# A graph layer on one core: a slot's rows and terms are made two and four chunks earlier, the list's words are packed in fewer VectorE instructions, and VectorE takes a share of the one-hots from the list's making on

## The chip, the cores and the metric

The kernel runs on one core of one Trainium2 chip. The core has five engines with a queue each: PE (TensorE, matmul), DVE (VectorE), ACT (ScalarE), POOL (GpSimd) and SP (SyncE, which only issues transfers). Each engine works off its own queue strictly in order, and an instruction whose input is not there holds up everything behind it in that queue. The metric is the device time of one execution in microseconds.

## The reference

```python
def _L0_gnn_ref(x, src, dst, theta_w, theta_b, phi_w, phi_b):   # x (6250, 256), 100000 edges sorted by dst
    x_src = x[src]
    x_dst = x[dst]
    theta_x = (x_dst - x_src) @ theta_w.T + theta_b
    phi_x = x_src @ phi_w.T + phi_b
    e = jax.nn.relu(theta_x + phi_x)
    out = jax.ops.segment_max(e, dst, num_segments=x.shape[0])
    return jnp.where(jnp.isfinite(out), out, 0.0)
x = _layernorm(x + _L0_gnn_ref(...), axis=-1)
```

The sum inside the relu splits into a term of the edge's target, and B[src] with B = x (phi - theta)^T. So the kernel makes the table B once (`b_rows` in DRAM), takes for every node the maximum of B over its incoming edges, and adds the rest at the end.

## The kernel before

The maxima are made in three ways, by three engines, at the same time.

*Part 1* (618 nodes, 81 steps): POOL gathers rows of B for 128 chunks of the sorted edges, and DVE runs a running maximum over them, one `scalar_tensor_tensor` of 128x256 a step (L696, helper `run_steps`). Results go to `maxima_1` (SP, L711).

*Slots* (the other 5632 nodes, 44 to a partition): the rows of B are cut into 17 slots of 383. In each slot every node may take one of its edges; `choice` (L1020 on, DVE, two slots a call) picks it for all nodes. The chosen row numbers are turned by PE (L1053), copied by ACT (L1055) and stored (SP, L1056, `chosen_rows`). Later PE fetches the chosen rows of a slot by matmul with one-hot matrices: `slot_halves(s, c)` does chunk c (1024 nodes, the sixth 512) of slot s. For a chunk, SP loads `want` (L1094); the one-hots `hot` are made block by block, three blocks, either by DVE in one comparison (L1100) or by ACT in an Abs for each block (L1102) and one Relu over all of ACT's blocks (L1105). `dve_hots[0]` says how many blocks DVE makes: 0 at first, 1 from late in the list's making on, 0 again near the end. PE then multiplies (L1113), 12 matmuls for each of two halves of 512-wide columns, from `terms`, which is the slot's rows `raw` (loaded by SP, L1078, one buffer) split into a rounded part (ACT, L1082) and its rest (DVE, L1083); `slot_terms` does this at the head of a slot's chunk 0. `terms` and `hot` have two buffers each, PSUM three. The result is copied to `acc` in slot 0 (ACT, L1122) and merged by maximum in the others (DVE, L1124). Chunks are dealt out in halves by `fetch_parts` and `fetch_half`.

*List* (part 2): edges that no slot took are packed into a list, 256 steps of 128 rows. `list_pieces` makes it on DVE: which table places are left over (L1213, L1215), a running count (L1216), sums over partitions by two PE matmuls (L1151, L1152), the words (node, row and distance to move in one integer, L1225 to L1237), eleven rounds of moves that close the gaps (L1244 to L1254), the store (L1263), and three gathers that fetch each partition its run (L519). After each `yield` of `list_pieces` the program emits a group of part 1 and a chunk, or a chunk alone; so the program order of that stage is: a piece of the list, eight steps of part 1, a chunk. Then POOL gathers the list's rows (L526 from `list_src`), each gather followed by a `pause` iota; DVE runs the list's steps two groups of eight behind, and `halves_until` spreads the remaining halves evenly over the list steps, so that 12 halves are left for the end (`SPREAD` 0.97: the last of the others is emitted at step 248 of 256). With `pinned` set, DVE's order of steps and of L1124 is the program's. The ends of part 1's chunks are merged by `tails_1` and `heads_1` (PE transposes L905 and L914, DVE L907 and L910, ACT L916).

At the end POOL gathers the nodes' maxima (44 gathers), PE makes the targets' term, and DVE and ACT do the layer norm.

The order on each engine is made when the program is built: a scheduler takes instructions by program order where they are ready by its reckoning, so an instruction can stand ahead of others that were written earlier. Where the code says `behind_in_order`, the order is forced.

## Time and profile before

| | us |
|---|---|
| three runs | 739.37, 734.26, 736.09 (median 736.09) |
| the profiled execution, its own time | 738.83 |
| its span, first to last instruction | 737.0 |
| busy in the span: PE, DVE, ACT, POOL | 661.5, 630.5, 532.7, 529.1 |
| mean granted TensorE clock | 0.955 of full speed |
| edge table and choice on DVE; PE makes B | 0 to 118 |
| the list's making on DVE, chunks on the side | 118 to 214 |
| the list is stored and its runs fetched | 214 to 228 |
| list gathers, list steps and 148 halves | 228 to 651 |
| the nodes' maxima, the end | 651 to 737 |

Times in the profile are us from the span's start, busy times are the length of an instruction from its start to its end; instructions of one engine are pipelined and overlap a little, so that the next starts before the one ahead has ended. A wait stands in square brackets behind the instruction, with what ended it. "PE x24" are matmuls: 24 make one full chunk, 12 a narrow one.

### The profile page before, as it was taken

The numbers are of one execution on the slowest core, as the hardware profiler recorded it, in microseconds if no ns is written. First come the engines' busy times: TensorE is split into PE (matmuls) and PEld (weight loads), VectorE is DVE, ScalarE is ACT, GpSimd is POOL, SyncE is SP. The second block draws the span as 40 slices with busy tenths as digits, with TensorE's granted clock in tenths as the row PEclk, the third lists the DMA queues.
The fourth block names the chain that finished last, engine by engine and source line by source line (L and its number), as shares of the span: only waits on it lengthen the run. The fifth ranks groups of instructions, "written<-read, shape, count | busy, mean of one in ns | idle before, by whom it ended". The sixth has DMA issues, their size and how long they took to land.

```text
span 737.0 us, 9895 instructions
## 1 busy us (share of the span) xinstructions
PE 661.5 (90%) x2908; PEld 536.1 (73%) x2908; DVE 630.5 (86%) x1193; ACT 532.7 (72%) x611; POOL 529.1 (72%) x730
## 2 busy tenths in 40 slices
PE   5989978679697999999999999999999988979990
PEld 3878756567475888888888888888888876758880
DVE  7999998999996678988989888888888984697885
ACT  1445788788697676967869687876877878852685
POOL 6810477888315848888888888888888888438880
PEclk9999998889798999999999999999999998989995
DMA  8997553737456547777787968786867675555874
GB/s 260 313 360 289 191 165 108 261 101 229 156 194 207 179 143 223 247 217 260 222 277 217 354 218 272 249 312 223 263 211 252 210 243 177 164 187 172 269 279 192
DMA packets 60879, 167.06 MB, mean 227 GB/s; under 512 B 11896, under 2 KB 21905, under 8 KB 54673
## 3 DMA queue, kind: packets, MB, share of 16 engines
q1 hardware_dynamic: 39717, 107.15, 41.6%
q0 software_dynamic: 18976, 52.35, 24.1%
q10 hardware_dynamic: 2124, 6.84, 2.5%
q8 instruction: 25, 0.41, 0.2%
q14 instruction: 37, 0.30, 0.1%
HBM read 102.94 MB, written 63.36 MB: 226 GB/s over the span
## 4 chain that ended last, share of the span: by engine, by line
PE 63%; DVE 11%; DMA 7%; ACT 7%; POOL 6%; issue 6%; SPq 0%; DVEq 0%; POOLq 0%; ACTq 0%
PE ps_f L1113 56%; PE ps_b L791 4%; POOL g L526 4%; DMA x_columns<-x_t 3%; DVE g L696 2%; ACT hot L1102 2%; ACT hot L1105 2%; DMA g<-maxima,place 2%; POOL pause L496 1%; DVE wide L1032 1%; DMA dst_w<-list_words,run_start 1%; DVE words L1244 1%; DVE acc L1124 1%; DMA w_in<-in_L_gnn_theta_w_dram 1%; ACT x_t L779 1%
## 5 line engine op out<-in xcount | busy, mean ns | idle before, releaser
L1113 PE MATMUL ps_f<-hot,terms 128*128 128x512 f32 x2156 | 519.9, 402 | 28.0 <-ACT hot L1105 22.0
L1113 PEld LDWEIGHTS ps_f<-hot,terms 128*128 128x128 f32 x2156 | 412.7, 194 | 128.8 <-ACT hot L1105 31.6
L526 POOL DMA_INDIRECT g<-b_rows,list_src x256 | 258.2, 1009 | 61.0 <-issue 37.3
L1102 ACT ACTIVATE hot<-want,minus_row 128x1024 fp32r<-128x1024 f16 (+1 forms) x224 | 229.0, 1071 | 97.7 <-PE ps_f L1113 97.7
L1124 DVE TENSOR_TENSOR acc<-acc,ps_f 128x1024 f32<-128x1024 f32 x192 | 215.8, 1129 | 69.4 <-PE ps_f L1113 68.6
L1105 ACT ACTIVATE hot<-hot 128x2048 fp32r<-128x2048 f32 (+2 forms) x102 | 196.4, 1925 | 2.5
L696 DVE SCALAR_TENSOR_TENSOR g<-g,caps 128x256 f32<-128x256 f32 x335 | 161.1, 481 | 2.1
L526 POOL DMA_INDIRECT g<-b_rows,src x65 | 89.4, 1376 | 62.8 <-DMA b_rows<-b_sb 43.0
L496 POOL IOTA pause<- 128x160 f32 x312 | 96.9, 311 | 2.3
L791 PE MATMUL ps_b<-weights,x_t 128*128 128x256 f32 x260 | 60.9, 388 | 2.8 <-ACT x_t L779 2.4
L526 POOL DMA_INDIRECT g<-maxima,place x44 | 42.7, 971 | 27.1 <-DMA maxima<-g 20.2
L791 PEld LDWEIGHTS ps_b<-weights,x_t 128*128 128x128 f32 x260 | 48.9, 194 | 11.3 <-ACT x_t L779 5.2
L1100 DVE TENSOR_SCALAR hot<-want,row_id 128x1024 fp32r<-128x1024 f16 (+1 forms) x70 | 52.1, 745 | 0.3 <-issue 0.3
L1363 PE MATMUL ps_e<-weights,kept 128*128 128x256 f32 x176 | 41.6, 379 | 0.0
L1393 ACT ACTIVATE squares<-x_f,r 128x256 bf16<-128x256 f32 x49 | 24.2, 494 | 20.6 <-DVE r L1390 20.6
L1363 PEld LDWEIGHTS ps_e<-weights,kept 128*128 128x128 f32 x176 | 33.4, 190 | 4.3
L794 ACT COPY b_sb<-ps_b 128x512 f32<-128x512 f32 (+1 forms) x25 | 14.4, 578 | 23.4 <-PE ps_b L791 16.8
L779 ACT COPY x_t<-ps_xt 128x512 f32<-128x512 f32 (+1 forms) x33 | 18.5, 588 | 13.1 <-PE ps_xt L776 7.8
L526 POOL DMA_INDIRECT g<-in_x_dram,src x16 | 23.1, 1444 | 5.4 <-issue 4.1
L1408 ACT ACTIVATE x_f<-x_f,r 128x256 f32<-128x256 f32 x41 | 21.4, 588 | 6.8 <-DVE r L1400 3.9
L1373 DVE TENSOR_TENSOR g<-g,ps_e 128x512 f32<-128x512 f32 x22 | 15.1, 686 | 8.7 <-DMA g<-maxima,place 3.5
L519 POOL DMA_INDIRECT dst_w<-list_words,run_start x3 | 3.1, 1048 | 25.8 <-DMA list_words<-work 25.5
(255 smaller groups left out, 429.6 us busy)
## 6 DMA issues: line engine op xcount, KB each, us to landing
maxima<-g SPq DMA_DIRECT2D x42, 1024.0 KB
want<-chosen_rows SPq DMA_DIRECT2D x85, 256.0 KB
x_q<-in_x_dram SPq DMA_DIRECT2D x12, 512.0 KB
b_rows<-b_sb ACTq DMA_DIRECT2D x12, 512.0 KB
x_columns<-x_t SPq DMA_DIRECT2D x22, 256.0 KB
kept<-x_columns SPq DMA_DIRECT2D x11, 512.0 KB
raw<-b_rows SPq DMA_DIRECT2D x16, 256.0 KB
g<-b_rows,list_src POOLq DMA_INDIRECT x256, 4.3
```

The source lines that it names most:

```text
L496: return nc.gpsimd.iota(t, pattern=[[step, t.shape[1]]], base=base, channel_multiplier=per_partition, allow_small_or_imprecise_dtypes=True,)
L526: one = nc.gpsimd.indirect_dma_start(out=to, out_offset=None, in_=table, in_offset=bass.IndirectOffsetOnAxis(ap=offsets, axis=0))
L696: one = nc.vector.scalar_tensor_tensor(g[:, k, :], last[part], caps[:, t : t + 1], g[:, k, :], op0=ALU.min, op1=ALU.max)
L779: nc.scalar.copy(x_t[:, :w], ps[:, :w])
L791: nc.tensor.matmul(ps[:, h, :], x_t[:, h, k, :], weights[:, k, 0, :], start=(k == 0), stop=(k == KC - 1))
L1100: nc.vector.tensor_scalar(hot[:, b, :], want, row_id[:, b : b + 1], None, op0=ALU.is_equal)
L1102: nc.scalar.activation(hot[:, b, :], want, AF.Abs, bias=minus_row[:, b : b + 1], scale=1.0)
L1105: nc.scalar.activation(apart, apart.bitcast(FP), AF.Relu, bias=1.0, scale=-1.0)
L1113: nc.tensor.matmul(ps[:, w : w + 512], terms[:, part, b, h * P : (h + 1) * P], hot[:, b, w : w + 512], start=(i == 0), stop=(i == n - 1),)
L1124: one = nc.vector.tensor_tensor(to, to, ps, op=ALU.max)
L1363: nc.tensor.matmul(a[:, i, :], x_t[:, 2 * i + c, :], weights[:, c, 1, :], start=False, stop=(i == w - 1 and c == KC - 1))
L1393: nc.scalar.activation(squares, x_f[:, k, :], AF.Square, bias=mean[:, k : k + 1], scale=1.0, accum_out=var[:, k : k + 1])
```

## The change

Seven edits, of which some lie far from each other in the program.

1. `slot_terms` becomes a generator in two steps. The loads of the next slot's `raw` are issued at chunk 2 of the slot before (`ROWS_AT`), and its two parts of `terms` are made at chunk 4 (`TERMS_AT`). Only slot 0 still does both at its chunk 0.
2. `dve_hots[0] = DVE_HOTS` is set ahead of the list's making instead of at its 14th piece: 13 chunks of the list's making and three behind it get one of their three blocks of one-hots from DVE.
3. The list: "empty" in one instruction instead of "left over" in two, the words in two instead of five, the owner in one instead of two. The addition of the node's number to the words (DVE, L1228) goes to POOL, as an addition and a cast, right behind the edge table.
4. `choice`: the first slot writes `unused` itself instead of multiplying it in. The memsets of `unused` (what is left of it) and of `words` go from DVE to POOL.
5. The sums' matmuls (L1151, L1152 before) are written one piece later, and are forced behind the latest chunk's last product.
6. The transposes of part 1's carries (L914 before) and their copy go from `tails_1` into `heads_1`, where they are forced behind the latest product as well.
7. In the last list groups `halves_until` is no longer called, and the last `fetch_parts` takes all that is left.

Its core, cut:

```diff
+ROWS_AT = 2
+TERMS_AT = 4
...
+    def heads_1(capped):
         carry = misc()
         for k in range(KC):
-            nc.tensor.transpose(carry[:, k * P : (k + 1) * P], capped[:, k, :], ident)
+            one = nc.tensor.transpose(carry[:, k * P : (k + 1) * P], capped[:, k, :], ident)
+            behind_in_order(one, latest_product[0], "slots ahead of the heads")
...
-    nc.vector.memset(unused, 1)
+    nc.gpsimd.memset(unused[:, CHOICE_R * TILES :], 1)
...
-        nc.vector.memset(words[:, : TR - W], EMPTY)
+        nc.gpsimd.memset(words[:, : TR - W], EMPTY)
...
+        by_nodes = words.rearrange(by_node, r=R)
+        nc.gpsimd.tensor_tensor(by_nodes, by_nodes, node_part.to_broadcast([P, TILES, R]), op=ALU.add)
+        nc.gpsimd.tensor_copy(word, words)
...
         terms = terms_of[s] = slots.tile([P, PARTS, KB, D], FR, name="terms")
...
-        if c == 0:
-            slot_terms(s)
+        if c == 0 and s == 0:
+            for _ in slot_terms(s):
+                pass
+        if c == ROWS_AT and s + 1 < NS:
+            terms_ahead[0] = slot_terms(s + 1)
+            next(terms_ahead[0])
+        if c == TERMS_AT and s + 1 < NS:
+            next(terms_ahead[0])
...
-        nc.vector.scalar_tensor_tensor(left_over, padded, float(SLOT * NS), unused, op0=ALU.is_lt, op1=ALU.mult)
-        valid, count = work_1, work_2
-        nc.vector.tensor_copy(valid.rearrange(by_node, r=R), left_over.rearrange("p (r j) -> p j r", r=R))
-        nc.vector.tensor_tensor_scan(count, valid, valid, 0.0, ALU.add, ALU.max)
+        empty, before_it = work_1, work_2
+        of_nodes = lambda flags: flags.rearrange("p (r j) -> p j r", r=R)
+        nc.vector.scalar_tensor_tensor(
+            empty.rearrange(by_node, r=R), of_nodes(padded), float(SLOT * NS), of_nodes(unused), op0=ALU.is_ge, op1=ALU.is_ge
+        )
+        nc.vector.tensor_tensor_scan(before_it, empty, empty, 0.0, ALU.add, ALU.max)
...
-        nc.vector.tensor_tensor(distance, order, count, op=ALU.subtract)
-        nc.vector.tensor_scalar(mask, valid, -1.0, None, op0=ALU.mult)
-        nc.vector.tensor_tensor(
-            word.rearrange(by_node, r=R),
-            words.rearrange(by_node, r=R),
-            node_part.to_broadcast([P, TILES, R]),
-            op=ALU.add,
-        )
-        nc.vector.tensor_scalar(distance, distance, 20, None, op0=ALU.logical_shift_left)
-        nc.vector.tensor_tensor(done, word, distance, op=ALU.bitwise_or)
-        nc.vector.tensor_tensor(done, done, mask, op=ALU.bitwise_and)
+        nc.vector.scalar_tensor_tensor(distance, empty, 0.5, before_it, op0=ALU.is_lt, op1=ALU.mult)
+        nc.vector.scalar_tensor_tensor(
+            done, distance, 20, word, op0=ALU.logical_shift_left, op1=ALU.bitwise_or
+        )
...
+    dve_hots[0] = DVE_HOTS
     for i, _ in enumerate(list_pieces()):
         if i == 14:
-            dve_hots[0] = DVE_HOTS
...
             list_steps(i, k)
-            halves_until(i * STEPS + k + 2)
...
-    fetch_parts(LAST_CHUNKS)
+    fetch_parts(len(CHUNKS) * NS)
```

What this does to the engines' orders at three places follows. Line numbers of the changed kernel are its own: its L1133 is L1113 before (a slot's matmuls), its L699 is L696, its L1120 is L1100, its L1145 is L1124, its L1094 is L1083, its L1264 and L1274 are L1244 and L1254.

PE around the end of part 1; the 240 matmuls are the chunks from the eighth to the last of slot 2. L905 turns the last step of part 1, L914 (after: L920) its capped tails; `ps_f` is a slot's product. Before:

```order
L858 MATMUL ps<-ids_158,hot_1465 128x83
L1113 MATMUL ps_f<-hot,terms 128x512 x240
L905 MATMUL ps<-ident,g 128x128 x2
L914 MATMUL ps<-ident,capped 128x128 x2
L1113 MATMUL ps_f<-hot,terms 128x512 x564
```

After:

```order
L861 MATMUL ps<-ids_158,hot_1462 128x83
L1133 MATMUL ps_f<-hot,terms 128x512 x216
L908 MATMUL ps<-ident,g 128x128 x2
L1133 MATMUL ps_f<-hot,terms 128x512 x96
L920 MATMUL ps<-ident,capped 128x128 x2
```

The second pair of transposes moved behind 96 matmuls (four chunks), and nothing stands between the first pair and the next chunk.

DVE where the list's words are made, behind the sums over partitions; `hot<-want` is one block of a chunk's one-hots. Before:

```order
L1225 TENSOR_TENSOR order<-order,work_775 128x1584
L1175 SCALAR_TENSOR_TENSOR number<-number,ends 128x3
L1179 TENSOR_SCALAR bad<-ends 128x1
L1226 TENSOR_SCALAR work_775<-work_774 128x1584
L1176 TENSOR_SCALAR run_start<-number 128x3
L1235 TENSOR_SCALAR order<-order 128x1584
L855 TENSOR_SCALAR hot_1357<-columns,low 128x128
L1236 TENSOR_TENSOR work_774<-words,order 128x1584
```

After:

```order
L1255 SCALAR_TENSOR_TENSOR work_774<-order,words 128x1584
L1200 TENSOR_SCALAR ends<-ends,chunk_1257 128x4
L1120 TENSOR_SCALAR hot<-want,row_id 128x1024
L1201 SCALAR_TENSOR_TENSOR number<-number,ends 128x3
L1205 TENSOR_SCALAR bad<-ends 128x1
L1264 TENSOR_SCALAR words<-work_774 128x1583
L1202 TENSOR_SCALAR run_start<-number 128x3
L1120 TENSOR_SCALAR hot<-want,row_id 128x512
```

Wide instructions are gone, and one-hots of the fifth and sixth chunk stand among the list's work.

DVE where `terms` of slot 2 is made. Before, behind the seventh to ninth rounds of moves (128x1520, 128x1456) and the last merge of slot 1 (the two of 128x512):

```order
L1254 COPY_PREDICATED work_774<-words,work_774 128x1520
L696 SCALAR_TENSOR_TENSOR g<-g,caps_171 128x256
L1124 TENSOR_TENSOR acc<-acc,ps_f 128x512
L696 SCALAR_TENSOR_TENSOR g<-g,caps_171 128x256
L1124 TENSOR_TENSOR acc<-acc,ps_f 128x512
L696 SCALAR_TENSOR_TENSOR g<-g,caps_171 128x256
L1244 TENSOR_SCALAR words<-work_774 128x1456
L696 SCALAR_TENSOR_TENSOR g<-g,caps_171 128x256
L1254 COPY_PREDICATED work_774<-words,work_774 128x1456
L696 SCALAR_TENSOR_TENSOR g<-g,caps_171 128x256
L1083 TENSOR_TENSOR terms<-raw,terms 128x768
```

After:

```order
L1274 COPY_PREDICATED work_774<-words,work_774 128x1552
L699 SCALAR_TENSOR_TENSOR g<-g,caps_171 128x256
L1145 TENSOR_TENSOR acc<-acc,ps_f 128x1024
L699 SCALAR_TENSOR_TENSOR g<-g,caps_171 128x256
L1094 TENSOR_TENSOR terms<-raw,terms 128x768
L699 SCALAR_TENSOR_TENSOR g<-g,caps_171 128x256
L1145 TENSOR_TENSOR acc<-acc,ps_f 128x1024
L699 SCALAR_TENSOR_TENSOR g<-g,caps_171 128x256
L1120 TENSOR_SCALAR hot<-want,row_id 128x1024
```

`terms` of slot 2 moved from behind the move over 128x1456 to behind the one over 128x1552, two rounds earlier, and a merge of slot 1 now stands behind it.

46 lines of the change are left out of this document (28 added, 18 removed).

## The prediction

> **What bounds the kernel now.** I read the table by stages first, then the waits, then the single engines' timelines at the seams. The stage table's columns are the stretch, its length, the busy time of PE, PE's weight loads, VectorE, ScalarE and GpSimd (with counts), the granted clock, and the DMA share with GB/s.
>
> ```profile
> 118.00:214.00 96.00, 74.66 (x281) 57.07 (x280) 91.47 (x154) 78.39 (x84) 60.90 (x43) 0.86 0.53 177
> 235.00:605.00 370.00, 369.92 (x1617) 302.35 (x1617) 312.81 (x484) 285.81 (x249) 316.67 (x476) 0.99 0.73 239
> ```
>
> From 235 to 605 PE is busy for 369.92 of 370 us, at clock 0.99: each us by which it enters this stage sooner stays won, unless another engine falls behind. From 118 to 214, while the list is made, VectorE is the full one (91.47 of 96), and PE works for 74.66 at a granted clock of 0.86. So the change is worth what it does to the list's making on VectorE and to PE's entry into the long stage. The waits of these two engines there (us in total, times, longest):
>
> ```profile
> DVE acc L1124 <- PE ps_f L1113: 2.9, 4, 1.2
> DVE capped L893 <- PE ps L892: 1.7, 2, 1.2
> ...
> PE ps_f L1113 <- ACT hot L1105: 13.6, 10, 3.1
> PE ps L914 <- DVE capped L910: 5.1, 1, 5.1
> PE ps L1151 <- DVE src_w L1149: 3.8, 1, 3.8
> ```
>
> The first two are VectorE's from 118 to 214, the rest PE's from 118 to 236. VectorE loses 4.6 us to PE, PE 13.6 to ScalarE's one-hots, and PE stands 5.1 us at one pair of transposes. PE's timeline at this seam:
>
> ```profile
> 194.81 12.74 PE L1113 MATMUL ps_f<-hot,terms 128*128 128x512 f32 x44 [3.00 <-ACT hot L1105]
> 208.70 5.73 PE L1113 MATMUL ps_f<-hot,terms 128*128 128x512 f32 x24 [1.14 <-ACT hot L1105]
> 214.62 5.73 PE L1113 MATMUL ps_f<-hot,terms 128*128 128x512 f32 x24 [0.19 <-ACT hot L1105]
> 220.57 8.58 PE L1113 MATMUL ps_f<-hot,terms 128*128 128x512 f32 x36 [0.21 <-ACT hot L1105]
> 228.98 0.38 PE L905 MATMUL ps<-ident,g 128*128 128x128 f32 x2
> 234.43 0.69 PE L914 MATMUL ps<-ident,capped 128*128 128x128 f32 x2 [5.06 <-DVE capped L910]
> 234.77 10.45 PE L1113 MATMUL ps_f<-hot,terms 128*128 128x512 f32 x33
> ```
>
> **The change part by part.** *VectorE up to the list's store.* These are the prices (name, shapes, count, busy us, mean ns):
>
> ```profile
> L1100 DVE TENSOR_SCALAR hot<-want,row_id 128x1024 fp32r<-128x1024 f16 x59 | 46.7, 791 | 0.3 <-issue 0.3
> L1046 DVE TENSOR_TENSOR unused<-unused,wide 128x1056 int16<-128x1056 int16 x17 | 12.0, 706 | 0.5
> L1042 DVE TENSOR_TENSOR wide<-wide,at 128x2112 int16<-128x2112 int16 x8 | 10.0, 1253 | 0.0
> L1100 DVE TENSOR_SCALAR hot<-want,row_id 128x512 fp32r<-128x512 f16 x11 | 5.5, 497 | 0.0
> L1003 DVE SCALAR_TENSOR_TENSOR padded<-work,words 128x1584 int16<-128x1584 f32 x1 | 3.0, 3044 | 0.0
> L1215 DVE CAST work<-wide 128x1584 f32<-128x1584 int16 x1 | 1.9, 1914 | 0.0
> L1225 DVE TENSOR_TENSOR order<-order,work 128x1584 int32<-128x1584 f32 x1 | 1.8, 1803 | 0.0
> L1228 DVE TENSOR_TENSOR words<-words,node_part 128x1584 int32<-128x1584 f32 x1 | 1.8, 1802 | 0.0
> L1213 DVE SCALAR_TENSOR_TENSOR wide<-padded,unused 128x1584 int16<-128x1584 int16 x1 | 1.8, 1801 | 0.0
> L1237 DVE TENSOR_TENSOR work<-work,work 128x1584 int32<-128x1584 int32 x1 | 1.8, 1801 | 0.0
> L1236 DVE TENSOR_TENSOR work<-words,order 128x1584 int32<-128x1584 int32 x1 | 1.8, 1799 | 0.0
> L1235 DVE TENSOR_SCALAR order<-order 128x1584 int32<-128x1584 int32 x1 | 1.0, 979 | 0.0
> L1226 DVE TENSOR_SCALAR work<-work 128x1584 int32<-128x1584 f32 x1 | 1.0, 977 | 0.0
> ```
>
> Gone: the words' addition, 1.80. In the choice, one multiplication less (0.71) and one wide comparison cut in two (2 x 0.70 for 1.25): 0.56. The words: five instructions (1.80 + 0.98 + 0.98 + 1.80 + 1.80 = 7.36) become two, each priced as L1225 (3.60): 3.76. The flags: L1213 and L1215 (3.71) become one that reads two inputs across the node order. L1215 reads one such input and takes 1.91; L1003 reads two and takes 3.04, which is the same form of access, so I take 3.04 and save 0.67 (the other end, 1.80, saves 1.91). The owner: about 0.3. Together 7.1. The two memsets on VectorE I cost at nothing:
>
> ```profile
> 7.00 0.69 DVE L735 TENSOR_TENSOR w_in<-w_in 128x512 f32<-128x512 f32 x1 [2.50 <-DMA w_in<-in_L_gnn_theta_w_dram]
> ...
> 14.44 0.95 POOL L519 DMA_INDIRECT dst_w<-in_dst_dram,window  x1 [2.21 <-DVE ids L667]
> ...
> 37.31 1.48 POOL L496 IOTA order<- 128x1584 f32 x1
> ...
> 82.04 1.42 POOL L526 DMA_INDIRECT g<-b_rows,src  x1 [42.98 <-DMA b_rows<-b_sb]
> ```
>
> VectorE waits 2.50 us for the weights behind them, longer than they take, and on GpSimd they lie in front of a gather that waits 2.21 us anyway.
>
> Added: the order of the changed kernel puts eleven one-hot blocks of 1024 and two of 512 ahead of the list's store: 11 x 0.79 + 2 x 0.50 = 9.7. So VectorE's own work up to the store grows by 9.7 - 7.1 = 2.6 us.
>
> GpSimd's addition and cast run while VectorE begins the choice, the full engine; GpSimd itself is idle from 39 to 82, so only the effect on VectorE counts. No row shows GpSimd computing from two inputs. The nearest is its iota of the same 1584 columns, 1.48 us for one stream written, beside which VectorE's rows do not stretch: one end is 0. The other: five streams (two read and one written, one read and one written) at 1.48, with VectorE stopped for all of it, 7.4. I take 1.5, nearer to the iota.
>
> Against this stand VectorE's own waits, 4.6 us. They fall where PE lacks ScalarE's one-hots. With one block on VectorE, ScalarE needs 2 x 1.14 + 1.92 = 4.2 us for a chunk instead of 3 x 1.14 + 2.77 = 6.2; a chunk's 24 matmuls take 5.73:
>
> ```profile
> L1102 ACT ACTIVATE hot<-want,minus_row 128x1024 fp32r<-128x1024 f16 x186 | 203.8, 1144 | 82.2 <-PE ps_f L1113 82.2
> L1105 ACT ACTIVATE hot<-hot 128x2048 fp32r<-128x2048 f32 x59 | 113.1, 1917 | 1.4
> L1105 ACT ACTIVATE hot<-hot 128x3072 fp32r<-128x3072 f32 x21 | 58.2, 2770 | 0.4
> ```
>
> I take these waits as gone (the other end: they stay). Sum up to the store: 2.6 + 1.5 - 4.6 = **-0.5 us**.
>
> *Terms and rows ahead.* The chain of work shows the terms as a link, and ScalarE waits for the rows:
>
> ```profile
> 195.22 0.88 DVE terms L1083
> ...
> ACT terms L1082 <- DMA raw<-b_rows: 9.8, 3, 6.2
> ```
>
> Slot 2's terms now stand two rounds of moves earlier, the next load follows at once, and PE no longer has to wait for them there. But the one-hot of that chunk now comes from the same full VectorE, so I count only what lies behind the store: PE's waits 1.14, 0.19 and 0.21 for ScalarE, of which **-1.0** (ends 0 and -1.5). In the long stage PE waits for nothing, so the other 13 slots gain nothing.
>
> *Sums.* PE's 3.8 us at L1151 are not counted: the fifth chunk's first block now comes from VectorE behind the list's words, so PE stands there longer than before, by the order some ten us. That costs nothing as long as VectorE paces this stage.
>
> *Transposes of the carries.* PE goes from 229.36 (end of L905) to the next chunk without the 5.06 us wait and the 0.7 of the pair. That chunk's one-hots ended on ScalarE only at 233.28, so the edit alone would give about 1.5; with two blocks of three on a ScalarE that is ahead, I take **-5.6** (ends -1.5 and -5.8). The pair returns four chunks later, with its input made long before.
>
> ```profile
> 230.53 2.75 ACT L1105 ACTIVATE hot<-hot 128x3072 fp32r<-128x3072 f32 x1
> ```
>
> *The last list groups.* Nothing: at step 248 the rule leaves 148 x (1 - 248/248.3) = 0.2 halves beyond the last twelve, that is none, and from there on the engines' orders read alike.
>
> *GpSimd behind it.* The list's gathers follow each other at 1.41 us and would hold the end if they did not move too:
>
> ```profile
> 228.35 0.95 POOL L526 DMA_INDIRECT g<-b_rows,list_src  x1 [6.78 <-DVE dst_w L1281]
> 229.76 0.96 POOL L526 DMA_INDIRECT g<-b_rows,list_src  x1 [0.16 <-issue]
> ...
> 266.86 1.22 POOL L526 DMA_INDIRECT g<-b_rows,list_src  x1 [9.76 <-DVE g L696]
> ```
>
> The first comes with the store, 0.5 us sooner, but by the order one more one-hot block (0.79) and one more narrow merge now stand in front of the addresses' last instruction, about 1.4 us: 229.3. At 266.86 GpSimd waited 9.76 us for a step of VectorE that PE paces, so PE can be that much sooner before GpSimd paces. Less the 0.9 of the first gather, the cushion covers 7.1, with 1.8 left.
>
> Sum: 0.5 + 1.0 + 5.6 = 7.1 us. The profiled execution (738.83, span 737.0) would be 731.7; it lies 2.7 above the median of the three runs, 736.09, which becomes **729.0**.
>
> [...]
>
> **The rivals.** *GpSimd stops VectorE.* While GpSimd adds and casts, the choice stands: 7.4 instead of 1.5, so 729.0 + 5.9 = 734.9. [...] Against it: beside the iota nothing stretched. [...]
>
> *GpSimd paces the list.* If the first gather slips 5 us more behind the new one-hots, that is 3.2 beyond what the cushion has left: 732.2. For it: the merges in front of it wait for PE. Against it: PE is sooner too.
>
> *Slower: one-hots as a barrier.* VectorE's queue is strict, and a one-hot may have to wait for a buffer that PE still reads, or for its `want`; the list's moves behind it then wait too. With 13 blocks ahead of the store, 0.55 us a block eats the whole gain; at 1.2, what a merge waited at most, the time is 729.0 + 13 x 1.2 = 744.6. For it: VectorE is the full engine and PE stands long at the fifth chunk. Against it: in the long stage the same blocks waited 0.3 us in all (row of L1100).
>
> *More than that.* GpSimd costs VectorE nothing (-1.5), the flags' instruction takes 1.80 (-1.2), the ends of the other terms (-0.7): 725.6.
>
> **How the numbers follow.** Forecast 0.50 (726 to 732), more than that 0.13, GpSimd stops VectorE 0.18, GpSimd paces 0.06, slower 0.13. The time is the forecast's, 729.0. The range goes from 724 to 738: below lies half of "more", 0.065, above the slower case, 0.13. One per cent is 7.4 us, about what a measurement of this kernel can tell from no change: under 728.7 lie half of the forecast (0.25) and "more" (0.13), 0.38; within 1% the other half and both GpSimd cases, 0.49; slower by more 0.13.
>
> **What would show it.** VectorE's last instruction ahead of the list's store some half a us sooner; VectorE's waits for PE in the list's making under 2 us; VectorE's choice instructions hardly longer than before while GpSimd adds; PE without a gap behind part 1's first transposes, and its full stretch beginning near 228; the wait of GpSimd for a list step shrunk to some 2 us. I am wrong if PE's full stretch begins at 233 or later, or if it has gaps or GpSimd paces it. If it begins at 228 and the end does not move, the seam was not what bounded.

## The result, and the profile after

| | median of 20 runs | lowest to highest |
|---|---|---|
| before | 737.43 us | 734.26 to 740.26 |
| changed | 735.46 us | 731.77 to 738.15 |

The ratio is 0.9964 (95% interval 0.9948 to 0.998): 2.7 us faster (1.5 to 3.8), where 7.1 were forecast. The profiled execution took 736.34 us, its span is 734.5. Several parts of the change moved the time, in both directions, and the largest gain and the largest loss are each more than what is left (the runs below).

The two stages of the changed kernel in the table by stages (columns as in the prediction):

```profile
118.00:214.00 96.00, 67.42 (x271) 53.66 (x272) 93.66 (x164) 58.23 (x75) 73.96 (x44) 0.86 0.53 172
235.00:605.00 370.00, 369.72 (x1629) 301.95 (x1627) 321.49 (x528) 291.03 (x253) 322.80 (x484) 1.00 0.75 244
```

The long stage is as full as before. In the list's stage PE works 7.2 us less than before (67.42 for 74.66), VectorE 2.2 us more. The waits in it, of PE from 118 to 236 and of VectorE from 118 to 214:

```profile
PE ps_f L1133 <- DVE hot L1120: 20.9, 5, 10.7
PE ps L861 <- DVE hot L859: 6.1, 1, 6.1
PE ps L1063 <- DVE chosen L1048: 1.4, 1, 1.4
PE ps_f L1133 <- ACT hot L1125: 0.8, 1, 0.8
...
DVE hot L1120 <- PE ps_f L1133: 2.4, 1, 2.4
DVE acc L1145 <- PE ps_f L1133: 1.8, 3, 1.3
```

PE's waits for ScalarE are gone (0.8), and in their place stand 20.9 us for VectorE's one-hots. VectorE still waits 4.2 us for PE. PE's timeline over the same seam:

```profile
150.36 9.86 PE L1133 MATMUL ps_f<-hot,terms 128*128 128x512 f32 x36 [10.70 <-DVE hot L1120]
...
192.51 10.88 PE L1133 MATMUL ps_f<-hot,terms 128*128 128x512 f32 x36 [3.56 <-DVE hot L1120]
205.67 30.55 PE L1133 MATMUL ps_f<-hot,terms 128*128 128x512 f32 x132 [2.29 <-DVE hot L1120]
236.06 0.38 PE L908 MATMUL ps<-ident,g 128*128 128x128 f32 x2
236.39 22.05 PE L1133 MATMUL ps_f<-hot,terms 128*128 128x512 f32 x96
```

From 205.67 on there is no gap, and the 5.06 us in front of the transposes are gone. By the prediction's own mark (the full stretch begins near 228) this looks better than forecast. It isn't: PE comes to this point with work undone. The view that shows it is the table by stages for the one-hot products alone (stretch, its length, PE's busy time and the number of matmuls, clock, DMA share, GB/s), of the kernel before and then of the changed one:

```profile
96.00:150.00 54.00, 37.19 (x132) 0.86 0.56 179
150.00:200.00 50.00, 41.11 (x148) 0.85 0.53 171
200.00:250.00 50.00, 42.83 (x173) 0.93 0.59 194
250.00:600.00 350.00, 345.69 (x1507) 1.00 0.74 240
```

```profile
96.00:150.00 54.00, 25.89 (x96) 0.81 0.51 168
150.00:200.00 50.00, 41.56 (x154) 0.86 0.57 181
200.00:250.00 50.00, 47.49 (x207) 1.00 0.60 199
250.00:600.00 350.00, 345.69 (x1507) 1.00 0.75 243
```

From 250 to 600 both do 1507 matmuls: PE is full and makes up for nothing. So what counts is how many are done by 250. The changed kernel loses 36 ahead of 150 and wins 6 and 34 after it: 457 for 453 in this execution, and 469 in a second one (below). A chunk's 24 take 5.7 us, so a matmul is worth 0.24 us: 1 to 4 us, which is what the medians show.

VectorE's way to the list's store, which the forecast summed, became longer, not shorter: 160.1 us from the row that writes `padded` to the owners' row (59.32 to 219.39 in the second execution) for 154.1 before (59.14 to 213.28). The owners' row before, and in the second execution of the changed kernel:

```profile
213.28 0.48 DVE L1261 TENSOR_TENSOR work<-work,owner 128x316 int32<-128x316 int32 x1
```

```profile
219.39 0.48 DVE L1280 SCALAR_TENSOR_TENSOR work<-work,owner 128x316 int32<-128x316 int32 x1
```

In the execution of the tables above all of that lies 2.4 us later still, mostly because the gather of `dst_w` landed 1.6 us later; the second execution doesn't have it, so it isn't the change's.

### The profile page after: what moved, and what is told of

It reads as the page before. It is cut to its first block, busy times and chain, and to the rows that moved or that the text cites. A ratio compares the mean times of both kernels' runs of the same rounds, so it can differ in the third digit from the quotient of the medians.

```text
span 734.5 us, 9894 instructions
## 1 busy us (share of the span) xinstructions
PE 654.2 (89%) x2908; PEld 533.2 (73%) x2908; DVE 637.7 (87%) x1201; ACT 504.8 (69%) x595; POOL 540.3 (74%) x734
## 5 line engine op out<-in xcount | busy, mean ns | idle before, releaser
L1133 PE MATMUL ps_f<-hot,terms 128*128 128x512 f32 x2156 | 512.0, 398 | 31.8 <-DVE hot L1120 20.9
L1133 PEld LDWEIGHTS ps_f<-hot,terms 128*128 128x128 f32 x2156 | 410.0, 192 | 127.6 <-ACT hot L1125 14.9
L1122 ACT ACTIVATE hot<-want,minus_row 128x1024 fp32r<-128x1024 f16 (+1 forms) x208 | 213.6, 1073 | 109.3 <-PE ps_f L1133 106.7
L1145 DVE TENSOR_TENSOR acc<-acc,ps_f 128x1024 f32<-128x1024 f32 x192 | 215.8, 1129 | 59.4 <-PE ps_f L1133 58.3
L1125 ACT ACTIVATE hot<-hot 128x2048 fp32r<-128x2048 f32 (+2 forms) x102 | 184.1, 1805 | 2.5
L699 DVE SCALAR_TENSOR_TENSOR g<-g,caps 128x256 f32<-128x256 f32 x335 | 161.2, 481 | 2.1
L528 POOL DMA_INDIRECT g<-b_rows,src x65 | 99.5, 1531 | 35.5 <-issue 18.0
L794 PE MATMUL ps_b<-weights,x_t 128*128 128x256 f32 x260 | 62.4, 394 | 4.0 <-ACT x_t L782 3.6
L1120 DVE TENSOR_SCALAR hot<-want,row_id 128x1024 fp32r<-128x1024 f16 (+1 forms) x86 | 63.5, 739 | 2.7 <-PE ps_f L1133 2.4
L1017 POOL TENSOR_TENSOR words<-words,node_part 128x1584 f32<-128x1584 f32 x1 | 3.1, 3092 | 30.4 <-DVE padded L1008 30.4
L1143 ACT COPY acc<-ps_f 128x1024 f32<-128x1024 f32 (+1 forms) x12 | 11.2, 937 | 19.9 <-PE ps_f L1133 19.9
L528 POOL DMA_INDIRECT g<-in_x_dram,src x16 | 18.1, 1132 | 5.5 <-issue 4.1
```

Source lines behind the costliest of these rows:

```text
L528: one = nc.gpsimd.indirect_dma_start(out=to, out_offset=None, in_=table, in_offset=bass.IndirectOffsetOnAxis(ap=offsets, axis=0))
L699: one = nc.vector.scalar_tensor_tensor(g[:, k, :], last[part], caps[:, t : t + 1], g[:, k, :], op0=ALU.min, op1=ALU.max)
L794: nc.tensor.matmul(ps[:, h, :], x_t[:, h, k, :], weights[:, k, 0, :], start=(k == 0), stop=(k == KC - 1))
L1120: nc.vector.tensor_scalar(hot[:, b, :], want, row_id[:, b : b + 1], None, op0=ALU.is_equal)
L1122: nc.scalar.activation(hot[:, b, :], want, AF.Abs, bias=minus_row[:, b : b + 1], scale=1.0)
L1125: nc.scalar.activation(apart, apart.bitcast(FP), AF.Relu, bias=1.0, scale=-1.0)
```

## The experiments

I first asked what the parts do alone and what undoing them in the changed kernel does. Every ratio is to the kernel before on the same chip. The table gives the number of one-hot matmuls in the three stretches, ScalarE's wait at about 200 us for a slot's rows (a sign of something else, as the last runs show), and the ratio:

| kernel | 96 to 150 | 150 to 200 | 200 to 250 | sum | wait for rows | ratio (95%) |
|---|---|---|---|---|---|---|
| only_rows_ahead_2 | 132 | 172 | 188 | 492 | 0.44 | 0.9854 (0.9828 to 0.988) |
| only_list | 134 | 174 | 173 | 481 | - | 0.9895 (0.987 to 0.9921) |
| list_and_transposes | 132 | 170 | 180 | 482 | - | 0.9904 (0.988 to 0.9929) |
| hots_at_14 | 132 | 164 | 180 | 476 | - | 0.9907 (0.988 to 0.9934) |
| hots_at_4 | 132 | 137 | 213 | 482 | - | 0.9913 (0.9891 to 0.9936) |
| hots_at_2 | 126 | 149 | 206 | 481 | - | 0.9915 (0.9885 to 0.9946) |
| hots_at_0 | 107 | 159 | 207 | 473 | - | 0.9930 (0.9907 to 0.9953) |
| transposes_undone | 100 | 162 | 205 | 467 | - | 0.9967 (0.9945 to 0.9988) |
| changed_again | 101 | 163 | 205 | 469 | - | 0.9975 (0.9953 to 0.9998) |
| only_transposes_2 | 132 | 149 | 182 | 463 | 7.63 | 0.9978 (0.9958 to 0.9998) |
| gpsimd_twice | 96 | 149 | 208 | 453 | - | 0.9988 (0.997 to 1.0006) |
| before | 132 | 148 | 173 | 453 | 6.20 | 1 |
| only_hots | 109 | 156 | 182 | 447 | 5.72 | 1.0019 (1.0003 to 1.0035) |
| rows_undone | 100 | 165 | 177 | 442 | 9.79 | 1.0026 (1.0006 to 1.0046) |
| only_gpsimd | 132 | 139 | 161 | 432 | 7.24 | 1.0026 (1.0005 to 1.0047) |

The sum orders the kernels nearly as the times do (476 beside 482 is within what two executions of one kernel differ). From top to bottom it is 60 matmuls, 14 us, for 12.7 us of time.

### First four, on a slower chip

Here the kernel before took 761.63 us with a spread of 2%, so these four are told for their traces.

**add_on_vector** puts the words' addition back on VectorE, and **hots_late** the hots to the fifteenth piece:

```diff
-        nc.gpsimd.tensor_tensor(by_nodes, by_nodes, node_part.to_broadcast([P, TILES, R]), op=ALU.add)
-        nc.gpsimd.tensor_copy(word, words)
...
+        nc.vector.tensor_tensor(
+            word.rearrange(by_node, r=R), words.rearrange(by_node, r=R),
+            node_part.to_broadcast([P, TILES, R]), op=ALU.add)
```

```diff
-    dve_hots[0] = DVE_HOTS
     for i, _ in enumerate(list_pieces()):
         if i == 14:
+            dve_hots[0] = DVE_HOTS
```

> The changed kernel with the words' addition back on VectorE, in one operation ahead of the words' making; GpSimd's add and cast are gone. Theory: GpSimd's two instructions held VectorE. The choice's first rows return from 3.44 and 3.16 us to about 0.78 and 1.98 (3.8 us less), VectorE gets 1.8 us of addition, the list's store comes about 2 us earlier, and the time falls by 0 to 2 us, to 733.5 to 735.5. Rival: the rows are long for another reason (the tile's new order, the padded row): they stay long, the store comes 1.8 us later, and the time is 735.5 to 737.3.

0.9927 (0.9881 to 0.9973); the choice's rows are back at 0.78 and 1.98. As the theory has it, and more in time than it gave.

> The changed kernel with VectorE's one-hots from the list's fifteenth piece on, as before the change. Theory: the hots are what makes the list late. VectorE is rid of 9.7 us of hots and of the 2.4 us wait for the first of them, the store comes about 10 to 12 us earlier, but ScalarE makes all hots again and TensorE waits for it some 10 to 13 us as it did before: the time goes to 732 to 735. Rival: the early hots are what carried the gain that there is, TensorE loses more to ScalarE than it lost to VectorE, and the time is 737 or more.

0.9998 (0.9962 to 1.0035), which is 737.3 us at the 737.43 of the kernel before: the rival's side, as far as this chip tells. The store does come 16 us sooner than in the changed kernel (144.0 us behind `padded`, for 160.1), but ScalarE's hots hold PE for 23.4 us instead: a first sign that the store's time is not what is paid.

**only_transposes** and **only_rows_ahead** are the kernel before with one part of the change each (the core of the two edits, cut):

```diff
+            one = nc.tensor.transpose(carry[:, k * P : (k + 1) * P], capped[:, k, :], ident)
+            behind_in_order(one, latest_product[0], "slots ahead of the heads")
```

```diff
-        if c == 0:
-            slot_terms(s)
+        if c == 0 and s == 0:
+            for _ in slot_terms(s):
+                pass
+        if c == ROWS_AT and s + 1 < NS:
+            terms_ahead[0] = slot_terms(s + 1)
+            next(terms_ahead[0])
+        if c == TERMS_AT and s + 1 < NS:
+            next(terms_ahead[0])
```

> The kernel before with one part of the change: the carries' transposes stand behind the pieces of the chunk that is ahead of them on TensorE. Theory (the third term of the forecast): the 5.06 us wait and the 0.6 us around it are gone, 5.6 us less than before, 731.8. Rival: TensorE fills the hole with matmuls that then are missing a little later, so only the lower end, 1.5 us, stays: 735.9. None of it: 737.4.

1.0031 (0.9989 to 1.0072): nothing, as far as this chip tells.

> The kernel before with one part of the change: a slot's rows are fetched two chunks and its terms made four chunks into the slot ahead. Theory: ahead of the full stretch it takes 1 to 1.5 us of TensorE's waits away, inside it nothing: 736 to 737.4. Rival: with the terms' rows ahead TensorE's waits at each slot's start go, 3 us or more: 734.4 or less.

0.9944 (0.9898 to 0.9991): the rival's side, and so the theory that I held was weak here already.

### The changed kernel with a part undone

**changed_again** is the changed kernel. **rows_undone** and **transposes_undone** take back what the two diffs above show. **hots_at_2** has the addition on VectorE as in add_on_vector, and

```diff
-    dve_hots[0] = DVE_HOTS
     for i, _ in enumerate(list_pieces()):
+        if i == 2:
+            dve_hots[0] = DVE_HOTS
```

> The changed kernel itself, as the mark for the other three on the same chip. Both theories: a ratio to the kernel before of 0.995 to 0.998 once more; the row that first writes the slots (128x1584, from the edge table) begins near 60 and not at 61.7, since that moment hung on one transfer of the profiled execution.

734.8 for 737.83 us, 0.9975; `padded` begins at 59.32. Both as expected.

> The changed kernel with a slot's rows and terms made at the slot's first chunk, as before the change. Theory: the rows ahead carry the gain; without them TensorE waits 3 to 4 us more ahead of 250 us and the ratio to before is 1.000 or more, 0.004 over the changed kernel. Rival (the forecast's second term, 1.0 us): the ratio lies within 0.002 of the changed kernel's.

740.19 us, 1.0026. The theory: the rows are worth 0.5% inside the change, some 4 us, not 1.

> The changed kernel with the carries' transposes where they were, ahead of the chunk's pieces. Theory: alone the transposes' move gained nothing, because TensorE then waited for ScalarE's hots at the same place; with VectorE's hots and the rows ahead nothing else is late there, so taking the move back costs 3 to 5 us, a ratio 0.004 to 0.007 over the changed kernel's. Rival: the move is worth nothing here either, and the ratio lies within 0.002 of the changed kernel's.

736.26 us, 0.9967: the theory falls, but the run tells less than I meant it to. The order of PE's instructions is the same with and without this part, because the rows ahead already put the transposes 96 matmuls back.

> The changed kernel with the words' addition on VectorE and VectorE's hots from the list's third piece on instead of from its beginning. Theory: the first of the changed kernel's waits of TensorE for VectorE's hots, 10.7 us, comes from a hot that stands behind the list's words on VectorE; two pieces later ScalarE makes that hot, the wait falls to 5 us or less, TensorE is 3 us or more further at 250 us than with the addition alone moved, and the ratio to before is 0.988 or less. Rival: ScalarE's hots are as late there (4 to 6 us, as in the kernels without the early hots), and the ratio stays at 0.991 to 0.995.

732.5 us, 0.9915. PE's longest wait for a hot falls from 10.7 to 7.33 us, less than expected; the ratio lies at the rival's edge.

### When VectorE's hots begin, and GpSimd

**hots_at_0** is the kernel of add_on_vector on a quiet chip, **hots_at_4** has `i == 4`, **hots_at_14** `i == 14`. **only_hots** is the kernel before with the hots from the list's start.

> The changed kernel with the words' addition back on VectorE and VectorE's hots from the list's making on, as in the changed kernel: a first look at it was on a chip whose runs spread over 2%, and here it is the mark for hots from later pieces. Theory: the ratio to before is 0.993 to 0.995, some 2.5 us better than the changed kernel, because the choice ends 2 us sooner and TensorE begins the hots' matmuls 5 us sooner. Rival: addition on VectorE or on GpSimd is the same, 0.997.

732.49 us, 0.9930: the theory.

> The changed kernel with the words' addition on VectorE and VectorE's hots from the list's fifth piece on. Theory: a smaller share of the list's chain waits behind hots, the store comes 1 to 2 us earlier than with hots from the third piece, and TensorE's longest wait for a VectorE hot falls below 7.3 us; ratio 0.988 to 0.991. Rival: ScalarE, which makes three blocks' hots of these chunks, is as late as in the kernel before, and the ratio goes back to 0.994 or more.

731.84 us, 0.9913, just above the theory's range; the longest wait for a VectorE hot is 3.5 us. The store comes 3 us later than with hots from the third piece (156.8 us behind `padded`, for 153.6), not 1 to 2 sooner, and the time is the same.

> The kernel before with one part of the change: VectorE's hots from the list's making on. Theory: the first hot stands as a barrier in the choice (2.4 us), the hots' 10 us lie in the list's chain, whose store comes 8 to 12 us later, and without the rows ahead and the shorter list nothing pays for it: ratio 1.003 to 1.008. Rival: TensorE gains at ScalarE's waits what VectorE loses, ratio 0.997 to 1.000.

739.16 us, 1.0019 (0.2 to 2.6 us slower): the theory's sign, below its size. The store comes 7.0 us later (161.1 us behind `padded`, for 154.1).

> The changed kernel with the words' addition on VectorE and VectorE's hots only from the list's fifteenth piece, as before the change: the end of the row of hots from the first, third and fifth piece (0.993, 0.9915 and 0.9913). Theory: without VectorE's hots ScalarE holds TensorE, 18 to 25 us of waits ahead of 250 us, and the ratio goes back to 0.996 to 1.000 although the store comes 10 us earlier. Rival: with the rows ahead ScalarE is in time, and the shorter list carries on: 0.990 or less.

732.27 us, 0.9907: the theory falls and the rival's 0.990 is just missed; it is as good as with hots from the third or fifth piece. The early hots move matmuls from one stretch to another (101 and 205, 132 and 180) and gain nothing. Where the 36 went is this row of PE in the changed kernel's second execution (it ends with the view, at 152 us, and has nine of the 36). In hots_at_4, where ScalarE makes that hot, the same 36 stand 15 us sooner:

```profile
148.03 4.21 PE L1133 MATMUL ps_f<-hot,terms 128*128 128x512 f32 x9 [10.71 <-DVE hot L1120]
```

```profile
132.56 11.36 PE L1130 MATMUL ps_f<-hot,terms 128*128 128x512 f32 x36 [1.09 <-ACT hot L1122]
```

VectorE comes to that hot only behind the list's words (L1255, then the hot, in the profiled execution of the changed kernel):

```profile
147.72 1.79 DVE L1255 SCALAR_TENSOR_TENSOR work<-order,words 128x1584 int32<-128x1584 int32 x1
149.43 0.22 DVE L1200 TENSOR_SCALAR ends<-ends,chunk 128x4 f32<-128x4 f32 x1
149.56 0.74 DVE L1120 TENSOR_SCALAR hot<-want,row_id 128x1024 fp32r<-128x1024 f16 x1
```

**gpsimd_twice** does GpSimd's addition twice, first into a table that is free; **only_gpsimd** is the kernel before with the addition and cast on GpSimd and nothing else.

```diff
+        nc.gpsimd.tensor_tensor(work_2.rearrange(by_node, r=R), by_nodes, node_part.to_broadcast([P, TILES, R]), op=ALU.add)
         nc.gpsimd.tensor_tensor(by_nodes, by_nodes, node_part.to_broadcast([P, TILES, R]), op=ALU.add)
```

> The changed kernel with GpSimd's addition of the words done twice, the first time into a table that is free then. Theory: VectorE stands for most of what GpSimd works there, so that the choice's first rows (3.44 and 3.16 us now) grow by 2.6 to 3.1 us in all, the flags begin that much later, and the ratio is 0.002 to 0.005 above the changed kernel's. Rival: the long rows come from something else in the choice, they stay as they are, and only the cast and the words come 3.1 us later, which nobody waits for: no difference.

738.03 us, 0.9988; the span is 736.0 for changed_again's 732.8. The long rows of the choice stay at 3.44 and 3.16, but only because the first addition found another instruction to stop: it began at 58.12, as soon as the words were there, and L965, which takes 0.98 otherwise, took 3.52. The choice begins 2.5 us later. In the trace that is the theory, at another place than it said; in the time it is not shown, since the ratio lies only 0.0013 above changed_again's, less than the theory's 0.002, and the intervals overlap. VectorE's and GpSimd's rows:

```profile
59.09 3.52 DVE L965 TENSOR_SCALAR work<-work 128x1584 f32<-128x1584 f32 x1
...
58.12 3.64 POOL L1017 TENSOR_TENSOR work<-words,node_part 128x1584 f32<-128x1584 f32 x1 [23.47 <-DVE words L1005]
65.86 3.04 POOL L1018 TENSOR_TENSOR words<-words,node_part 128x1584 f32<-128x1584 f32 x1 [4.10 <-DVE padded L1008]
```

> The kernel before with the words' addition and cast on GpSimd behind the slots' table, and nothing else. Theory: VectorE stands 3.8 us in the choice and is rid of 1.8 us of addition; the store comes 2 us later, TensorE starts its first chunk later: ratio 1.002 to 1.005. Rival: GpSimd's work lies beside VectorE's and the addition is saved: 0.997 to 0.999.

740.62 for 738.77 us, 1.0026 (0.4 to 3.5 us slower), the theory. PE's first chunk starts at 99.35 instead of 95.72. The same rows in the kernel before and in the changed kernel, with GpSimd's beside them:

```profile
62.22 0.78 DVE L1028 TENSOR_SCALAR wide<-padded 128x1056 int16<-128x1056 int16 x2
62.91 1.80 DVE L1228 TENSOR_TENSOR words<-words,node_part 128x1584 int32<-128x1584 f32 x1
64.63 1.98 DVE L1032 TENSOR_TENSOR wide<-wide 128x1056 int16<-128x1056 int16 x5
```

```profile
64.88 3.44 DVE L1036 TENSOR_SCALAR wide<-padded 128x1056 int16<-128x1056 int16 x2
68.35 3.16 DVE L1040 TENSOR_TENSOR wide<-wide 128x1056 int16<-128x1056 int16 x5
...
64.93 3.09 POOL L1017 TENSOR_TENSOR words<-words,node_part 128x1584 f32<-128x1584 f32 x1 [30.44 <-DVE padded L1008]
68.09 1.59 POOL L1018 CAST words<-words 128x1584 int32<-128x1584 f32 x1
```

VectorE stands 2.66 and 1.18 of GpSimd's 3.09 and 1.59 us, to save an instruction of 1.80.

### The list, the rows and the transposes alone

**only_list** is the changed kernel with all the edits undone that were shown so far (hots, rows, transposes, addition), so that the list's fewer operations, the choice's first slot and the two fillings on GpSimd are left. Left in it are also edits 5 and 7 (the sums' matmuls one piece later, the last list groups), which no run takes alone. **list_and_transposes** puts the transposes' diff back. The other two are the same kernels as only_transposes and only_rows_ahead, on quieter chips.

> The kernel before with the list's part of the change alone: the flags, count, positions, words and owners in fewer operations, the choice's first slot without a product, two fillings on GpSimd. The words' addition stays on VectorE, the hots, rows and transposes as before. Theory: VectorE is 4 to 6 us shorter up to the list's store (7.1 us of the forecast less the addition's 1.8), the store comes that much earlier, but TensorE waits for ScalarE's hots as before and gains at most 1 us: ratio 0.998 to 1.000. Rival: the list's chain holds TensorE in the seam, and the time falls by the whole 4 to 6 us: 0.992 to 0.995.

731.47 for 738.58 us, 0.9895: 7.8 us (5.8 to 9.6). My theory falls, and the rival's mechanism is not it either, as the next runs show. The later sums can have given little of it by themselves: up to 150 us PE has done 134 matmuls for 132, and the gain comes behind that (174 for 148 from 150 to 200).

> The kernel before with the transposes' move alone once more, since its first runs were on a chip whose runs spread over 2%. Theory: nothing, ratio 0.998 to 1.001, because the wait is taken over by ScalarE's hots at the slot's first chunk, which end some 1.5 us ahead of where the transposes' wait ended. Rival (the forecast's third term): 5.6 us, 0.9925.

736.52 us, 0.9978: 1.6 us (0.1 to 3.1), the lower end of the forecast's term. PE's wait is taken over by ScalarE's hots (PE's row, then ScalarE's that it waited for):

```profile
233.79 11.55 PE L1115 MATMUL ps_f<-hot,terms 128*128 128x512 f32 x43 [4.06 <-ACT hot L1107]
...
230.98 2.75 ACT L1107 ACTIVATE hot<-hot 128x3072 fp32r<-128x3072 f32 x1
```

> The list's part alone (0.9895) with the transposes' move. Theory: the list's part keeps the 5.1 us wait of TensorE for the carries; moved, it is taken over by ScalarE's hots, which end 1 to 2 us sooner, so the ratio is 0.987 to 0.990. Rival (the forecast's third term, now that nothing else is late): the whole 5 us, 0.983.

731.22 for 738.77 us, 0.9904: the transposes add nothing to the list. PE's wait of 5.11 us at the pair, as in only_list, is gone, and one of 3.72 us for a VectorE hot stands there instead.

> The kernel before with the rows and terms ahead of a slot alone, a second time (the first was on a chip whose runs spread over 2%). Theory, formed from the traces so far: four kernels show ScalarE waiting 5.7 to 9.8 us at about 200 us for a slot's rows (the kernel before 6.20), whose load waits for VectorE's subtraction of the slot ahead, which stands behind the list's moves; these four are the slowest. The rows ahead take that wait away and nothing else, so the time falls by 3 to 5 us: ratio 0.993 to 0.996. Rival (the forecast's second term): 1 us, 0.9985.

727.97 for 738.77 us, 0.9854: 10.8 us (8.9 to 12.7), more than twice the theory's 3 to 5, and the fastest of all kernels here. One part alone beats the whole change by 8 us. What it took away is first this, in the kernel before (PE's rows, with a weight load, then VectorE's row that the weight load waits for, then ScalarE's):

```profile
188.90 0.91 PE L1113 MATMUL ps_f<-hot,terms 128*128 128x512 f32 x2 [2.58 <-ACT hot L1105]
190.60 1.22 PE L1113 MATMUL ps_f<-hot,terms 128*128 128x512 f32 x2 [0.79 <-DVE acc L1124]
196.14 10.99 PEld L1113 LDWEIGHTS ps_f<-hot,terms 128*128 128x128 f32 x42 [0.82 <-DVE terms L1083]
...
195.11 0.97 DVE L1083 TENSOR_TENSOR terms<-raw,terms 128x768 fp32r<-128x768 f32 x1
...
200.96 0.83 ACT L1082 CAST terms<-raw 128x768 fp32r<-128x768 f32 x1 [6.20 <-DMA raw<-b_rows]
202.61 3.23 ACT L1102 ACTIVATE hot<-want,minus_row 128x1024 fp32r<-128x1024 f16 x3 [0.82 <-PE ps_f L1113]
```

and in the kernel with the rows ahead alone:

```profile
189.23 5.95 PE L1125 MATMUL ps_f<-hot,terms 128*128 128x512 f32 x24 [1.40 <-ACT hot L1117]
...
183.63 0.94 DVE L1086 TENSOR_TENSOR terms<-raw,terms 128x768 fp32r<-128x768 f32 x1
...
192.73 0.84 ACT L1085 CAST terms<-raw 128x768 fp32r<-128x768 f32 x1 [0.44 <-DMA raw<-b_rows]
```

VectorE's subtraction makes the second part of slot 2's `terms`, and it stands in the middle of the list's moves. Until it ends at 196.08, PE can do only the first two of each twelve matmuls, which need the rounded part alone: six from 188.90 on (two, two, and two more at 194.81), where the kernel with the rows ahead does 24 from 189.23 to 195.18. From 190 to 200 us the two kernels do 14 and 38 one-hot matmuls, 24 matmuls or 5.7 us of PE's work apart. PE keeps what it has won: a small matmul behind its full stretch (the check of `n_bad`) stands at 596.78 us for 605.49.

ScalarE's wait of 6.20 us hangs on the same subtraction: there is one `raw`, and the next slot's rows can be fetched only when VectorE has read the last slot's. But that wait is not what PE pays for here. Behind it ScalarE waits another 0.82 us until PE gives back a buffer of one-hots, so rows that came sooner by themselves would have started the next hots no earlier. (In only_transposes_2 and rows_undone no such wait follows; there the rows' wait may cost something of its own.)

Five kernels of the table have ScalarE's wait, and they are the five with the fewest matmuls from 150 to 250 (300 to 342; the others have 344 to 368). In these five the subtraction begins between 194.9 and 202.7 us, in the other ten between 171.5 and 190.0. The list's part alone moves it from 195.1 to 171.5 us, from behind the eighth round of moves into the fifth. By the traces that is how the list's part gains without the rows ahead, and why the two don't add up; no run moves the subtraction and nothing else.

The second wait is the transposes'. PE's timeline at the seam with the rows ahead alone:

```profile
224.67 0.44 PE L907 MATMUL ps<-ident,g 128*128 128x128 f32 x2 [2.12 <-DVE g L698]
226.84 23.68 PE L1125 MATMUL ps_f<-hot,terms 128*128 128x512 f32 x96 [1.73 <-ACT hot L1117]
250.36 0.38 PE L916 MATMUL ps<-ident,capped 128*128 128x128 f32 x2
```

The transposes stand 96 matmuls later here too, though nothing was done to them, and PE enters the full stretch at 226.84 instead of 234.77.

Five of these kernels form a chain that leads from the kernel before to the changed one, with one part more in each: the list 0.9895, with the transposes 0.9904, with the rows ahead 0.9907 (hots_at_14), with VectorE's hots from the list's start 0.9930 (hots_at_0), with the addition on GpSimd 0.9975 (changed_again). So the list's part (with edits 5 and 7) gains 7.8 us, the transposes and the rows add nothing to it, the early hots cost 1.7 us (their intervals overlap) and GpSimd's addition 3.3 us. The order matters: in the changed kernel the rows ahead are worth some 4 us (rows_undone), since there, with the early hots and GpSimd's hold, the subtraction is late again without them (202.7 us, for 187.0 with them).

## Why the prediction was wrong, point by point

**What failed** are two terms of the sum, and the measure under them.

*Transposes*, the largest term: "with two blocks of three on a ScalarE that is ahead, I take -5.6". Taking the move back in the changed kernel changes nothing (0.9967 for 0.9975), because the rows ahead already put the pair 96 matmuls later.

*GpSimd's addition*: the step is "I take 1.5, nearer to the iota". VectorE stands 3.84 us, and with the addition back on VectorE the kernel is 0.45% faster, 3.3 us (hots_at_0 for changed_again).

*The measure*: "each us by which it enters this stage sooner stays won". PE's stretch without a gap begins at 205.67, earlier than the 228 of the forecast, and the time falls by 2.7 us, not by 7.1. PE enters it behind: by 200 us it has done 250 one-hot matmuls, the kernel before 280. From 250 on PE is full in both kernels, so what counts is the number done by then.

**Sums.** The 10.7 us at the fifth chunk came as the order said. By 150 us the early hots leave PE 23 to 25 matmuls short (109 in only_hots and 107 in hots_at_0, for 132), with GpSimd's hold 31 to 36, some 8 us. Most of them are made up by 250: hots_at_14, which doesn't have this wait, has 180 from 200 to 250 where hots_at_0 has 207, and is 1.7 us faster, with intervals that overlap. So "costs nothing" was not far off, but not for the reason given there, that VectorE paces the stage.

**VectorE up to the store: -0.5 forecast, +5.9 measured** (160.1 for 154.1). Its pieces, from the same two rows: the list 147.2 for 154.1, that is -7.0 (without the addition priced at 5.3); the hots 158.2 in hots_at_0 for 147.4 in hots_at_14, +10.8 (priced 9.7); GpSimd 160.1 for 158.2, +1.9 (1.5 - 1.8 = -0.3 priced). VectorE's waits of 4.6 us, taken as gone, are 4.2 after. So two of the four were wrong: the waits, and GpSimd, where I took 1.5 and VectorE stands 3.84. The time does not follow the store, though: the rows ahead alone gain 10.8 us with a store that comes 2.6 us later (156.8), the list's part 7.8 us with one that comes 6.9 sooner. The flags cost 3.68, not 3.04, and save nothing:

```profile
125.39 3.68 DVE L1240 SCALAR_TENSOR_TENSOR work<-padded,unused 128x1584 f32<-128x1584 int16 x1
```

**Terms and rows ahead: -1.0 forecast, -10.8 alone, about -4 inside the change.** The prediction saw that PE no longer has to wait for the terms there, and counted only the small waits behind the store, since the next hot would come from the full VectorE. Alone, the wait for the terms is 5.7 us of the 10.8, by the matmuls counted above. This is the term most mis-sized, on the other side.

**Transposes: -5.6 forecast, -1.6 alone, nothing inside the change.** The row of ScalarE's hots that ended at 233.28 stood in the prediction and gave 1.5; I took the upper end. The 5.06 us did go, but the rows ahead take them.

**What would show it** named the store half a us sooner (5.9 later), VectorE's waits for PE under 2 us (4.2) and the choice hardly longer (3.84): each was wrong, and each of them could be read without looking at the seam, where alone the profile looked as forecast.

**What held**: the long stage is unchanged; the two memsets and the last list groups show nothing in the traces; GpSimd does not pace, its cushion shrank from 9.76 to 1.16 us (forecast about 2):

```profile
266.06 1.22 POOL L528 DMA_INDIRECT g<-b_rows,list_src  x1 [1.16 <-DVE g L699]
```

**The rivals**: "GpSimd stops VectorE" (734.9) was half of the matter: 0.45% between hots_at_0 and changed_again, 3.3 us, where it gave 5.9. That its time lies 0.6 us from the measured 735.46 is in part luck, since its sum keeps the 5.6 us of the transposes. "One-hots as a barrier" had the right mark, one hot in the choice that waits 2.36 us for PE, at a tenth of its price (1.7 us for 15.6).

What stays open: why the list's part on top of the rows ahead (hots_at_14, 0.9907) is slower than the rows ahead alone (0.9854). Its trace shows the places, not the cause: PE waits 3.72 us at 226.97 for a hot that VectorE makes behind its 3.87 us wait for the list's gathered words, and ScalarE keeps PE waiting 4.29 us at 187. Both waits stand in list_and_transposes too, so they come with the list's part. Open is also what the later sums' matmuls give, and why GpSimd's addition seems to cost more with late hots (0.9998 in hots_late on the slower chip, 0.9907 in hots_at_14 without it). The rows ahead with VectorE's hots from about 200 us on, where these win most (205 to 213 matmuls for 188), wasn't tried.

## What to carry to other kernels

When one engine is full from some point to nearly the end, count what it has done by that point, in every version; an earlier store or a shorter chain on another engine is worth nothing until that count rises. Before pricing parts one by one, ask which wait each of them removes: the rows ahead took away two waits, and the list's part and the transposes each one of the same two, so their gains (10.8, 7.8 and 1.6 us alone) did not add up. And a short instruction that another engine needs, deep in a full engine's queue, is a wait in the making: here a subtraction of 0.97 us. The longest wait in the profile need not be the one that is paid; look at what the waiting engine would have waited for next.

## What was not expected of the hardware

Three rows of VectorE took longer beside GpSimd's: one of instructions with two inputs and two of instructions with one. With two: five int16 minima, 3.16 us beside the cast of 1.59 in the changed kernel, 1.98 in the kernel before. With one: a pair of int16 exclusive-ors, 3.44 us beside the addition of 3.09 in the changed kernel, 0.78 before, and a float32 addition of constants, 3.52 us beside the addition of 3.64 in gpsimd_twice, 0.98 before. And an instruction that reads two int16 inputs across the node order takes 3.68 us for 1584 columns, as long as the two instructions in its place (1.80 and 1.91), while the row with two inputs of float32 and an int16 output took 3.04.

PE's granted clock is lower in and behind some of its gaps: in the kernel before it is 0.52 from 190 to 200 us, where the one-hot products keep PE busy for 6.30 of 10 us, and 1.00 from 200 to 210; in the changed kernel it is 0.50 from 139 to 150, with PE busy for 0.66 us. It isn't so at every gap: in the kernel before, from 180 to 190, with 6.70 us busy, it is 0.96. Where the clock was lower, a wait cost more than its length: the 36 matmuls behind the wait of 10.70 us took 9.86 us in the changed kernel, at a clock of 0.85, and the 36 of the kernel before at 133.78, ahead of which PE had done only six small matmuls since 128.22, took 10.47 us at 0.79; 36 behind a wait of 0.21 us took 8.58 us at 1.00 (the kernel before, at 220.57).
